# Scores inside the feature weights of a graph-attention kernel's set-up, and its first six adjacency steps prepared in the last set-up block

## The chip, the cores and the metric

The kernel runs on one core of a Trainium2 chip. The metric is the device time of one execution in microseconds. The engines are called PE (TensorE matmul), PEld (its weight loads), DVE (VectorE), ACT (ScalarE), POOL (GpSimd) and SP (SyncE). DMA transfers are issued from the queues of SP, ACT and POOL.

## What is computed

There are 4096 nodes with 512 features and a dense 0/1 adjacency matrix A. Two residual layers follow one another; the change touches the set-up of the first, a graph attention with 8 heads of 64 features.

```python
feats   = einsum('nf,hfo->hno', X, W)              # 8 heads x 64
s_self  = einsum('hno,ho->hn', feats, a_self)
s_neigh = einsum('hno,ho->hn', feats, a_neigh)
dense   = leaky_relu(s_self[:, :, None] + s_neigh[:, None, :], 0.2) * A
attn    = softmax(dense, axis=-1)
out     = relu(einsum('hij,hjo->hio', attn, feats) + b)   # then (N, 512)
x       = layernorm(x + out)
# second layer: attention inside 32 diagonal blocks of 128 nodes, again with
# a residual and a layernorm
```

## The kernel before

The work falls into a set-up (about the first 165 us) and four main passes, one for each pair of heads (`main_pass(0)` to `main_pass(3)`); the second layer runs in pieces between the steps of the last pass. PE's instructions stand in the order of the program (`manual_schedule`). The other engines' orders and those of the DMA queues are made by a scheduler from the program order and its own estimates.

**Set-up.** It goes over the 32 tiles of 128 nodes in eight blocks `k` of four tiles `u`. `load_rows(k)` (L608) brings four tiles of x on SP's queue, into a pool of four buffers. `turn_rows(k)` transposes them on PE (L652, 16 transposes) and ACT copies the result to `xT_f` (L655). `features(k, u)` (L734) multiplies a tile by the feature weights `w_sb_f`: four fp32 matmuls with 128x128 weights and 512 columns, which the trace shows as eight passes. DVE adds the bias from PSUM (L742). The head scores take a way of their own: `scores(k)` (L663) multiplies the transposed block by `wa`, the products of W with `a_self` and `a_neigh`; ACT copies the result to `st` (L671); `exponentials(k)` (L677) brings it back to columns by matmuls with `stack`, and takes five exps on ACT (L686 to L691) and some small bf16 parts on DVE (L694 to L708). `rows_of_exponentials` (L713) and `columns_of_exponentials` (L726) turn the results for later use: the rows go to DRAM as `pu_d`. `scaled_features(k, u)` makes two staging tiles, `gst` (features times an exponential, L748) and `fst` (features split into two float32r parts, L756 on ACT and L757 on DVE), each from a pool of three buffers, and stores them to `g_d` and `f_d` on POOL's queue (L769). The pools of PSUM are seven banks `ps_set` for the set-up and one `ps_m`. After blocks 3, 4 and 5 a part of A is loaded and cast to 8-bit floats on POOL's queue (`load_adjacency`, L587).

**Main pass.** A step `j` is one of 32 rows of tiles, for a chunk `c` of 1024 columns; passes 0 to 2 take eight steps at a time. In pass 0 `bring(0, c, j)` transposes two steps of A on PE (L1113, 16-bit pairs, into `ps_m`), ACT casts each to a float32r tile `at` (L1117), and POOL's queue stores it to `at_d` (L1118); later passes load `at_d` back. For a step DVE makes two tiles `q` (L1367: max, then product), ACT or DVE a `mark` from each (L1376, L1372), and PE sums `accf` (L1387, `at` by `f_s`), `acc` (L1407, `q` by `g_s`), `dens` (L1421, `mark` by `e_b`) and in pass 0 `ae` (L1331). `f_s` and `g_s` are loaded from `f_d` and `g_d`. The tiles `at` and `q` come from pools of 6, to which `ring` adds the further pools `more_at` (6) and `more_q` (2) in passes 0 to 2. At the very first step the pass itself calls `bring` for its eight steps.

Of the kernel before, what the change touches and what calls it, by code (L numbers as in the profile page):

```python
# [19 lines left out]
P = 128  # L20
# [384 lines left out]
def adjacency_streamed_path(  # L405
# [50 lines left out]
    const = ctx.enter_context(tc.tile_pool(name="fconst", bufs=1))  # L456
    first_pass = ExitStack()
# [25 lines left out]
    for c in range(FC):  # L483
# [6 lines left out]

    stack = const.tile([P, 2 * H], F32, name="stack")
    nc.vector.tensor_reduce(
        stack,
        ident.rearrange("p (c k) -> p k c", c=FC)[:, : 2 * H, :],
        AX.X,
        OP.add,
    )
# [56 lines left out]
    more = {}  # L554

    def ring(name, pool, n):

        if name not in more:
            return pool
        k = turns[name] % (n + more[name][1])  # L560
        turns[name] += 1
        return pool if k < n else more[name][0]

    def partial_sums(dst, wide, rhs):

        for c in range(FC):
            nc.tensor.matmul(
                dst[32 * c : 32 * c + 32, :], wide[:, c, :32], rhs[:, c, :], start=True, stop=True
            )
# [21 lines left out]

    with tc.tile_pool(name="setup1", bufs=1, side="right") as one, tc.tile_pool(
        name="setup2", bufs=2, side="right"
    ) as two, tc.tile_pool(name="setup3", bufs=3, side="right") as three, tc.tile_pool(
        name="xtp", bufs=4, side="right"
    ) as xtp, tc.tile_pool(name="ps_setup", bufs=7, space=PSUM) as pss:
        NB = NT // 4
        xts, xTs, sts, pu_js, rows = {}, {}, {}, {}, {}
# [13 lines left out]
        w_sb = one.tile([P, FC, H * FH], F32, name="w_sb_f")  # L612
        for c in range(FC):
            nc.scalar.dma_start(
                w_sb[:, c].rearrange("p (h o) -> p h o", h=H),
                W[:, ts(c, P), :].rearrange("h p o -> p h o"),
            )
        a_b2 = three.tile([P, PR, 2, FP], F32R, name="fst").bitcast(F32)
        a_b2 = a_b2.rearrange("p r s n -> p (r s n)").rearrange(
            "p (k h o) -> p k h o", k=2, h=H  # L620
        )
# [11 lines left out]
        wa = one.tile([P, FC, 32], F32, name="wa")  # L633
        nc.vector.memset(wa, 0.0)
        for c in range(FC):
            for k in range(2):
                prod = three.tile([P, H, FH], F32, name="fb")
                nc.vector.tensor_mul(
                    prod, w_sb[:, c].rearrange("p (h o) -> p h o", h=H), a_b2[:, k]
                )  # L640
                nc.vector.tensor_reduce(wa[:, c, k * H : (k + 1) * H], prod, AX.X, OP.add)
        xs = one.tile([P, FC, NB], F32, name="xs")

        def turn_rows(k):
# [4 lines left out]
            for u, c in order if k == 0 else sorted(order, key=lambda x: x[1]):  # L649
                if u == 0:  # L650
                    pts[c] = pss.tile([P, 4, P], F32, name="ps_set")
                nc.tensor.transpose(pts[c][:, u, :], xts[k][u][:, ts(c, P)], ident)  # L652
# [6 lines left out]
        def scores(k):  # L659

            ps = pss.tile([P, 4 * P], F32, name="ps_set")
            for c in range(FC):
                nc.tensor.matmul(  # L663
                    ps[32 * c : 32 * c + 32, :],
                    wa[:, c, :],
                    xTs[k][:, c].rearrange("p u n -> p (u n)"),
                    start=True,
                    stop=True,
                )
            st = sts[k] = one.tile([P, 4 * P], F32, name="st")  # L670
            nc.scalar.copy(st, ps)  # L671

        def exponentials(k):
            blk = slice(4 * k, 4 * k + 4)
            pts = pss.tile([P, 4, 2, H], F32, name="ps_set")
            for u in range(4):
                nc.tensor.matmul(  # L677
                    pts[:, u].rearrange("p k h -> p (k h)"),
                    tile_j(sts[k], u),
                    stack,  # L680
                    start=(u == 0),
                    stop=True,
                    skip_group_check=True,
                )
            s_c, t_c = pts[:, :, 0, :], pts[:, :, 1, :]
            nc.scalar.activation(e_all[:, blk, 1, :], t_c, AF.Exp)  # L686
            nc.scalar.activation(e_all[:, blk, 0, :], t_c, AF.Exp, scale=ALPHA)
            nc.scalar.activation(d_all[:, blk, :], t_c, AF.Exp, scale=ALPHA - 1.0)
            pu_j = pu_js[k] = two.tile([P, 4, 2, H], F32, name="pu_j")
            nc.scalar.activation(pu_j[:, :, 1, :], s_c, AF.Exp, scale=-ALPHA)  # L690
            nc.scalar.activation(pu_j[:, :, 0, :], s_c, AF.Exp, scale=1.0 - ALPHA)  # L691


# [16 lines left out]
        def rows_of_exponentials(k):  # L710
# [5 lines left out]
            row = rows[k] = one.tile([2 * H, 4 * P], F32, name="pu_row")  # L716
# [14 lines left out]
        def features(k, u):  # L731
            pf = pss.tile([P, H * FH], F32, name="ps_set")
            for c in range(FC):
                nc.tensor.matmul(  # L734
                    pf,
                    tile_j(xTs[k][:, c].rearrange("p u n -> p (u n)"), u),
                    w_sb[:, c, :],
                    start=(c == 0),
                    stop=(c == FC - 1),
                )  # L740
            fb = three.tile([P, H, FH], F32, name="fb")
            nc.vector.tensor_add(fb.rearrange("p h o -> p (h o)"), pf, b_row)  # L742
            return fb

        def scaled_features(k, u, fb):
            j = 4 * k + u
            gst = three.tile([P, PR, 2, FH], F32, name="gst")
            nc.vector.tensor_tensor(  # L748
                gst.rearrange("p r h o -> p (r h) o"),
# [4 lines left out]
            fst = three.tile([P, PR, 2, FP], F32R, name="fst")  # L754
# [10 lines left out]
            for dst, n, src in (  # L765
                (g_d, FP, gst.rearrange("p r h o -> p r (h o)")),
                (f_d, 2 * FP, fst.rearrange("p r s n -> p r (s n)").bitcast(F32)),
            ):
                nc.gpsimd.dma_start(dst[:, k, :, ts(u, n)].rearrange("r p n -> p r n"), src)  # L769

        turn_rows(0)
        for k in range(NB):
            if k + 1 < NB:
                load_rows(k + 1)
            fbs = [features(k, 0)]
            if k == 0:
                fbs.append(features(k, 1))
                scores(0)
            else:
                exponentials(k)  # L780
            if k + 1 < NB:
                turn_rows(k + 1)
            if k == 0:
                exponentials(0)
            scaled_features(k, 0, fbs[0])
            if k:
                fbs.append(features(k, 1))
                columns_of_exponentials(k - 1)
            scaled_features(k, 1, fbs[1])
            fbs.append(features(k, 2))  # L790
            scaled_features(k, 2, fbs[2])
            if k + 1 < NB:
                scores(k + 1)
            rows_of_exponentials(k)
            if k == NB - 1:
                xsum = one.tile([P, FC], F32, name="xsum")
                nc.vector.tensor_reduce(xsum, xs, AX.X, OP.add)
                xsum_b = one.tile([P, FC, 32], F32, name="xsum_b")
# [730 lines left out]
```

## Time and profile before

| | us |
|---|---|
| median of three runs | 2074.67 (2074.32 to 2076.41) |
| the profiled execution, its own time | 2074.4 |
| its span, first to last instruction | 2072.1 |
| PE busy in it | 2040.3 |
| DVE busy | 1663.9 |
| ACT busy | 1536.7 |

The mean granted TensorE clock is 0.996. The profile is of one execution. Busy times overlap between engines. A row of a group gives the line, engine and operation, the tiles written and read, and the count. In the chain of waits each piece is what the end of the program is traced back to. A fp32 matmul of the program stands as two records.

### The profile page before, as it was taken

How to read it: one execution, taken by the hardware profiler on the slowest of the kernel's cores; microseconds unless marked ns; L12 is line 12 of the kernel's file. 1: busy time of each engine (PE TensorE's matmuls, PEld its weight loads, DVE VectorE, ACT ScalarE, POOL GpSimd, SP SyncE). 2: the span in 40 equal slices, each digit the busy share in tenths (PEclk: the TensorE clock that was granted, in tenths of full speed). 3: DMA queues.
4: the chain of work that ended last, by engine and by line, in shares of the span. 5: the costliest groups of instructions: out<-in, count | busy, mean ns of one | idle time of the engine just before them, and what ended most of it. 6: DMA issues, size and time to landing. Idle time of an engine off the chain costs nothing.

```text
span 2072.1 us, 37981 instructions
## 1 busy us (share of the span) xinstructions
PE 2040.3 (98%) x14934; PEld 999.7 (48%) x14934; DVE 1663.9 (80%) x2058; ACT 1536.7 (74%) x1821; POOL 247.5 (12%) x393
## 2 busy tenths in 40 slices
PE   8999999999999999999999999999999999999997
PEld 4555555444445444444445444544454444545443
DVE  5557888888799998798999999999975984885654
ACT  3338898888878899788889889998885666567420
POOL 2343222222100000000000000000210210210111
PEclk9999999999999999999999999999999999999999
DMA  8999999999899999788999899989974763775211
GB/s 252 265 258 248 272 293 265 296 261 297 264 332 349 361 334 338 261 312 300 315 318 337 312 342 327 325 292 361 325 234 144 245 243 132 227 272 168 71 49 43
DMA packets 207881, 551.28 MB, mean 266 GB/s; under 512 B 25292, under 2 KB 66252, under 8 KB 207692
## 3 DMA queue, kind: packets, MB, share of 16 engines
q1 hardware_dynamic: 140748, 425.79, 59.4%
q0 software_dynamic: 62784, 121.91, 23.4%
q8 instruction: 119, 1.95, 0.4%
q10 hardware_dynamic: 4160, 1.05, 0.2%
q14 instruction: 70, 0.57, 0.1%
HBM read 491.79 MB, written 107.22 MB: 289 GB/s over the span
## 4 chain that ended last, share of the span: by engine, by line
PE 81%; DMA 8%; issue 5%; DVE 3%; ACT 2%; POOL 1%; POOLq 0%; SPq 0%; DVEq 0%; ACTq 0%
PE acc L1407 35%; PE accf L1387 20%; DMA at_d<-at 5%; PE ps_m L1050 5%; PE ps_m L978 5%; PE dens L1421 5%; PE ps_set L734 4%; DVE q L1367 1%; PE ps_m L1005 1%; PE ps_m L1064 1%; ACT mark L1376 1%; DMA xt_f<-in_x_dram 1%; PE ps_m L907 1%; PE ps_m L1113 1%; PE ps_m L958 1%
## 5 line engine op out<-in xcount | busy, mean ns | idle before, releaser
L1367 DVE SCALAR_TENSOR_TENSOR q<-p_row,d_all,at 128x1024 f32<-128x1024 f32 x1024 | 1242.6, 1280 | 159.2 <-PE acc L1407 130.1
L1376 ACT ACTIVATE mark<-q,nb_all 128x1024 fp8e4<-128x1024 f32 x896 | 994.2, 1145 | 173.1 <-DVE q L1367 158.1
L1407 PE MATMUL acc<-q,g_s 128*32 128x512 f32 x8192 | 903.3, 593 | 1.1 <-DVE q L1367 0.4
L1407 PEld LDWEIGHTS acc<-q,g_s 128*32 128x32 f32 x8192 | 264.6, 110 | 594.5 <-issue 533.7
L1387 PE MATMUL accf<-at,f_s 128*128 128x512 f32 x2048 | 493.3, 397 | 1.9 <-issue 1.8
L1387 PEld LDWEIGHTS accf<-at,f_s 128*128 128x128 f32 x2048 | 379.3, 188 | 110.6 <-issue 29.1
L1132 ACT ACTIVATE ck<-ck,neg_half_f 128x1024 f32<-128x1024 f32 x128 | 146.0, 1140 | 22.1 <-DMA ck<-in_adj_dram 22.1
L1133 ACT ACTIVATE ck<-ck,neg_quarter 128x1024 f32<-128x1024 f32 x128 | 146.3, 1143 | 1.9
L1117 ACT CAST at<-ps_m 128x1024 fp32r<-128x1024 fp8e4 x128 | 120.2, 1025 | 8.7 <-PE ps_m L1113 5.6
L1421 PE MATMUL dens<-mark,e_b 128*6 128x512 fp8e4 x2048 | 124.4, 379 | 0.7 <-ACT mark L1376 0.7
L734 PE MATMUL ps_set<-w_sb_f,xT_f 128*128 128x512 f32 x256 | 117.3, 607 | 0.1
L978 PE MATMUL ps_m<-x1T,M_sb 128*128 128x512 f32 x256 | 113.1, 595 | 1.6 <-ACT x1T L959 1.6
L1050 PE MATMUL ps_m<-wvT,x1T 128*128 128x512 f32 x256 | 114.2, 594 | 0.0
L1252 POOL DMA_DIRECT2D hs_d<-hst x12 | 10.7, 894 | 834.0 <-DVE hst L1242 740.0
L1372 DVE TENSOR_SCALAR mark<-q,d_all 128x1024 fp8e4<-128x1024 f32 x128 | 96.0, 750 | 5.1 <-DVE q L1367 0.5
L1421 PEld LDWEIGHTS <-e_b 128*6 128x6 bf16 x2048 | 52.8, 86 | 80.4 <-issue 37.0
L1118 POOL DMA_DIRECT2D at_d<-at x128 | 68.8, 538 | 170.5 <-ACT at L1117 106.9
L756 ACT ACTIVATE fst<-fb 128x512 fp32r<-128x512 f32 x32 | 20.3, 636 | 83.9 <-DVE fb L742 52.9
L978 PEld LDWEIGHTS ps_m<-x1T,M_sb 128*128 128x128 f32 x256 | 47.9, 190 | 63.0 <-issue 59.9
L1050 PEld LDWEIGHTS ps_m<-wvT,x1T 128*128 128x128 f32 x256 | 47.6, 190 | 57.2 <-issue 56.0
L985 ACT ACTIVATE zT<-ps_m,zb 128x512 f32<-128x512 f32 x32 | 21.8, 683 | 71.0 <-PE ps_m L978 71.0
L734 PEld LDWEIGHTS ps_set<-w_sb_f,xT_f 128*128 128x128 f32 x256 | 49.2, 200 | 51.5 <-issue 50.2
(185 smaller groups left out, 1117.9 us busy)
## 6 DMA issues: line engine op xcount, KB each, us to landing
at<-at_d SPq DMA_DIRECT2D x384, 512.0 KB, 6.1
ck<-in_adj_dram SPq DMA_DIRECT2D x128, 512.0 KB, 5.5
f_s<-f_d SPq DMA_DIRECT2D x128, 512.0 KB, 7.3
at_d<-at POOLq DMA_DIRECT2D x128, 512.0 KB, 14.9
g_s<-g_d SPq DMA_DIRECT2D x128, 256.0 KB, 5.7
f_d<-fst POOLq DMA_DIRECT2D x32, 512.0 KB, 8.5
p_row<-pu_d SPq DMA_DIRECT2D x32, 512.0 KB, 6.9
a_b<-in_adj_dram POOLq DMA_DIRECT2D x32, 512.0 KB, 16.4
```

What stands on the lines that cost most here:

```text
L734: nc.tensor.matmul(pf, tile_j(xTs[k][:, c].rearrange("p u n -> p (u n)"), u), w_sb[:, c, :], start=(c == 0), stop=(c == FC - 1),)
L978: nc.tensor.matmul(pz, L1["M"][:, f, ts(c, P)], x1T[:, f, :], start=(f == 0), stop=(f == FC - 1),)
L1050: nc.tensor.matmul(pv, x1T[:, f, ts(u, P)], L1["wvT"][:, f, :], start=(f == 0), stop=(f == FC - 1),)
L1117: nc.scalar.copy(at, both[:, :, k])
L1132: tc.keep_in_program_order(nc.scalar.activation(ck, ck, AF.Square, bias=neg_half))
L1133: nc.scalar.activation(ck, ck, AF.Abs, bias=neg_quarter, accum_out=binp[:, k : k + 1])
L1367: nc.vector.scalar_tensor_tensor(q, p_row[h], d_j, ats[r, c, j].bitcast(F32), op0=OP.max, op1=OP.mult)
L1372: nc.vector.tensor_scalar(mark, q, d_j, None, op0=OP.is_gt, saturate=False)
L1376: nc.scalar.activation(mark, q, AF.Sigmoid, bias=nb_all[:, j, hh : hh + 1], scale=BIG, saturate=False,)
L1387: nc.tensor.matmul(accf[:, s, :], f_s[j // 4][:, j % 4, w, :], ats[r, c, j][:, ts(s, HB)], start=(j == 0 and w == 0), stop=(j == NT - 1 an ...
L1407: nc.tensor.matmul(acc[o : o + 32, s, :], g_s[j // 4][:, j % 4, h, o % FH : o % FH + 32], qs[j, h][:, ts(s, HB)], start=(j == 0), stop=(j ...
L1421: nc.tensor.matmul(dens[lo : lo + 6, :], e_b[:, j, 2 * r + h, :], marks[j, h][:, ts(s, HB)], start=(j == 0), stop=(j == NT - 1),)
```

## The change

- The scores become part of the feature weights: `w_sb_f` has 66 columns for each head, 64 of features and two of scores (the sums over W times `a_self` and `a_neigh`). A tile's product is then 528 columns wide and lies in two PSUM banks (`ps_fe`, two buffers of two banks; `ps_set` keeps three). Each of the four matmuls is split into two of 264 columns. `scores`, the copy `st`, and the matmuls with `stack` are gone. The exps are taken for each tile from PSUM by two small DVE products with `powers` and three exps on ACT. The first three tiles are multiplied without the score columns, and get their scores from 12 small matmuls in `first_scores`.
- The two staging tiles of `scaled_features` come from the main pass's pools `q` (`both`: the biased features and `gst`) and `at` (`fst`), six buffers each. Their stores are issued on SP's queue.
- `rows_of_exponentials(k)` and `columns_of_exponentials(k)` run in the next block; those of the last block follow its last tile.
- `more_at` is opened before the set-up and used first by `ring`. In the last block `early_steps` calls `bring` for the steps 0 to 5 of the first pass, after the features of tiles 0, 1 and 2.

```diff
-    more = {}
+    more = {"at": (at2, MORE)}
...
-            return pool
-        k = turns[name] % (n + more[name][1])
+            return pool
+        pool_2, m = more[name]
+        k = turns[name] % (n + m)
         turns[name] += 1
-        return pool if k < n else more[name][0]
+        if name == "at":
+            return pool_2 if k < m else pool
+        return pool if k < n else pool_2
...
-    ) as xtp, tc.tile_pool(name="ps_setup", bufs=7, space=PSUM) as pss:
+    ) as two, tc.tile_pool(name="xtp", bufs=4, side="right") as xtp, tc.tile_pool(
+        name="setup_rows", bufs=1, side="right"
+    ) as late, tc.tile_pool(name="ps_setup", bufs=3, space=PSUM) as pss, tc.tile_pool(
+        name="ps_feat", bufs=2, space=PSUM
+    ) as psf:
...
         for c in range(FC):
+            prod = qp.tile([P, C], F32, name="q").rearrange("p (k h o) -> p k h o", k=2, h=H)
             for k in range(2):
+                nc.vector.tensor_mul(prod[:, k], w_sb[:, c, :, :FH], a_b2[:, k])
+                nc.vector.tensor_reduce(w_sb[:, c, :, FH + k], prod[:, k], AX.X, OP.add)
...
-        def scores(k):
-            ps = pss.tile([P, 4 * P], F32, name="ps_set")
-            for c in range(FC):
-                nc.tensor.matmul(
-                    ps[32 * c : 32 * c + 32, :],
-                    wa[:, c, :],
-                    xTs[k][:, c].rearrange("p u n -> p (u n)"),
-                    start=True,
-                    stop=True,
-                )
-            st = sts[k] = one.tile([P, 4 * P], F32, name="st")
-            nc.scalar.copy(st, ps)
...
+        def exponentials(k, u, sc):
+            j = 4 * k + u
+            if u == 0:
+                pu_js[k] = two.tile([P, 4, 2, H], F32, name="pu_j")
+            st = small.tile([P, 5, H], F32, name="st")
+            for lo, hi, w in ((0, 3, 1), (3, 5, 0)):
+                nc.vector.tensor_tensor(
+                    st[:, lo:hi].rearrange("p k (q h) -> p k q h", q=2),
+                    sc[:, None, :, :, w].to_broadcast([P, hi - lo, 2, H // 2]),
+                    powers[:, lo:hi].rearrange("p k (q h) -> p k q h", q=2),
+                    OP.mult,
+                )
+            nc.scalar.activation(e_all[:, j], st[:, 0:2], AF.Exp)
+            nc.scalar.activation(pu_js[k][:, u], st[:, 3:5], AF.Exp)
+            nc.scalar.activation(d_all[:, j, :], st[:, 2], AF.Exp)
...
         def features(k, u):
-            pf = pss.tile([P, H * FH], F32, name="ps_set")
+            pf = psf.tile([P, 2, HB], F32, name="ps_fe")
+            pf = pf[:, :, : H * FW // 2].rearrange("p q (h w) -> p q h w", w=FW)
+            scored = k > 0 or u == 3
+            cols = slice(0, FW if scored else FH)
             for c in range(FC):
-                nc.tensor.matmul(
-                    pf,
-                    tile_j(xTs[k][:, c].rearrange("p u n -> p (u n)"), u),
-                    w_sb[:, c, :],
...
+                for q in range(2):
+                    nc.tensor.matmul(
+                        pf[:, q, :, cols],
+                        tile_j(xTs[k][:, c].rearrange("p u n -> p (u n)"), u),
+                        w_sb[:, c, 4 * q : 4 * q + 4, cols],
...
+            both = qp.tile([P, C], F32, name="q").rearrange("p (s h o) -> p s h o", s=2, h=H)
...
+            if scored:
+                exponentials(k, u, pf[:, :, :, FH:])
+            return both
...
-            fst = three.tile([P, PR, 2, FP], F32R, name="fst")
+            fst = atp.tile([P, C], F32R, name="at").rearrange(
+                "p (r s n) -> p r s n", r=PR, s=2
+            )
...
-                nc.gpsimd.dma_start(dst[:, k, :, ts(u, n)].rearrange("r p n -> p r n"), src)
+                nc.sync.dma_start(dst[:, k, :, ts(u, n)].rearrange("r p n -> p r n"), src)
...
+        def early_steps(k, u):
+            if k == NB - 1 and u < 3:
+                bring(0, 0, 2 * u)
...
+            for u in range(4):
+                fbs[u] = features(k, u)
+                early_steps(k, u)
+                if u == (0 if k else 2) and k + 1 < NB:
+                    turn_rows(k + 1)
+                if u == 1 and k:
+                    rows_of_exponentials(k - 1)
+                if u == 2 and k:
+                    columns_of_exponentials(k - 1)
+                if u == 2 and k == 0:
+                    first_scores()
+                    for v in range(3):
+                        scaled_features(k, v, fbs[v])
+                if k or u == 3:
+                    scaled_features(k, u, fbs[u])
...
+            parts_of_exponentials(k)
...
                 if at_step == 0:
                     for j in cycle:
-                        bring(0, 0, j)
+                        if (0, 0, j) not in ats:
+                            bring(0, 0, j)
```

## The prediction

> **What bounds the kernel now.** I read the page's busy shares and chain of waits first, then a table of windows cut at the blocks of the set-up, then the chain and the timelines inside them. The page:
>
> ```profile
> PE 2040.3 (98%) x14934; PEld 999.7 (48%) x14934; DVE 1663.9 (80%) x2058; ACT 1536.7 (74%) x1821; POOL 247.5 (12%) x393
> PE 81%; DMA 8%; issue 5%; DVE 3%; ACT 2%; POOL 1%; POOLq 0%; SPq 0%; DVEq 0%; ACTq 0%
> ```
>
> TensorE is the bound nearly everywhere, so a microsecond taken off its set-up should reach the end. The windows (span, then busy time of PE, PEld, DVE, ACT and POOL with counts, clock, DMA share, GB/s) run from one block's second `features` call to the next; the last is the step from set-up into the main pass.
>
> ```profile
> 39.45:58.10 18.65, 18.65 (x75) 9.70 (x74) 10.24 (x27) 6.49 (x22) 6.67 (x10) 1.00 0.91 262
> 95.35:113.80 18.45, 18.45 (x74) 9.51 (x73) 7.33 (x15) 4.19 (x10) 5.70 (x8) 1.00 1.10 245
> 161.55:178.20 16.65, 13.91 (x97) 11.50 (x97) 12.74 (x15) 14.90 (x16) 7.60 (x12) 0.79 0.86 293
> ```
>
> A block costs 18.5 us with PE full, DVE and ACT half idle, and the DMA rings near full. The boundary has 2.7 us of PE idle and a clock of 0.79. One block in the chain of waits (start, us, what):
>
> ```profile
> 95.35 3.44 PE ps_set L734 x8
> 98.79 0.35 PE ps_set L726 x4
> 99.14 3.64 PE ps_set L734 x8
> 102.78 1.00 PE ps_set L663 x8
> 103.78 0.54 PE ps_set L713 x4
> 104.31 6.88 PE ps_set L734 x16
> 111.19 0.84 PE ps_set L677 x8
> 112.03 1.79 PE ps_set L652 x16
> ```
>
> It adds to 18.48: four feature tiles 13.96 (a tile is eight fp32 passes of 512 columns, 3.44, or 3.64 after a matmul of another weight shape), scores 1.00, `stack` 0.84, transposes 1.79, rows 0.54, columns 0.35.
>
> **The feature passes.** Each becomes two of 264 columns (256 of features, 8 of scores), with the 128x128 weights loaded twice as often; 512 columns show no price for that. The weight loads' timeline in the last pass (start, us) has three neighbours:
>
> ```profile
> 1703.18 0.19 PEld L978 LDWEIGHTS ps_m<-x1T,M_sb 128*128 128x128 f32 x1 [0.24 <-issue]
> 1703.61 0.19 PEld L978 LDWEIGHTS ps_m<-x1T,M_sb 128*128 128x128 f32 x1 [0.24 <-issue]
> 1713.68 3.52 PEld L1387 LDWEIGHTS accf<-at,f_s 128*128 128x128 f32 x16
> 1718.23 1.86 PEld L1005 LDWEIGHTS ps_m<-x1T,zT 128*128 128x128 f32 x16
> ```
>
> L978 streams 512 fp32 columns, one pass per 0.43. L1005 streams 128: (1.86-0.19)/15 = 0.111 a pass, so a 0.19 us load hides behind even that. A line through the two gives 0.224 at 264 columns. L1387, one pass per (3.52-0.19)/15 = 0.222, has the same load behind about as long a stream. Bounds: 0.220 (a straight share of 0.43) and 0.239 (L1387's mean over the page is 493.3/2048 = 0.241, with group changes in it). I take 0.224: a tile costs 16 x 0.224 = 3.58, 0.14 more than 3.44. The two ends move the set-up by 32 x 16 x (-0.004 to +0.015) = -2 to +8.
>
> The Trainium skill (TensorE: Matmul & The Clock Gate, LDWEIGHTS) gives a load of P columns P/1.2 ns, 107 for these, and its section on the back-to-back gap lets load and matmul together set the spacing, which speaks against halving the stream. Were 0.107 only half hidden, a pass would cost 0.28 and the set-up 27 us more; L1005's 0.111 with a load each time disagrees, so the trace decides.
>
> **A block.** Gone: scores 1.00 and `stack` 0.84. New: 4 x 0.14 = 0.57, and 0.2 for a second tile that follows another weight shape (after the rows; after the columns it was there). The 24 exps and products of a block are small: exps of 128x32 took 0.20 on ACT (6.5 of 18.6 busy), products are bounded by the 0.16 to 0.22 of DVE's small rows, eight of them 1.6 on an engine at 10. They hide behind the next tile's 3.6 us. So does the staging in `at` and `q` tiles: with three buffers ACT waited 23.1 us for `f_d` transfers without moving PE, and now there are six. With three `ps_set` buffers the fourth transpose group waits for ACT's first copy (0.60, started 0.65 after the first group): 0 to 0.2, I take nothing. So 18.48 - 1.84 + 0.57 + 0.2 = 17.4; six blocks save 6 x 1.05 = **6.3**.
>
> **The head.** Until the eighth weight product (20.1) PE now waits too, for `features(0,2)` needs the bank that the first addition on DVE frees (product rows end about 19.6, addition 0.69: 20.4). Then 3.5 + 1.8 (transposes) + 24 score passes of 16 columns at 0.112 (the `stack` rows: 0.84 for 8) 2.7 + 3.7 + 3.6 + 1.8 = 37.5 to 37.9 against 39.45 before: **-1.6**, bounds -2.2 to 0.
>
> **The last block.** From 148.96 to 161.55 it took 12.59. Now three tiles 10.74, rows 0.54, columns 0.35, L567 0.99, three weight-shape changes 0.6, three `bring` groups at 0.62 (the L1113 x8 of the chain) 1.9: 15.1, **+2.5**. Their six casts (1.02 each, 6.1 us) go to ACT, which was busy 3.4 of 12.6 there; without that cover each pair would hold the single `ps_m` bank for 2 us more. End of features: 161.55 - 1.6 - 6.3 + 2.5 = 156.1.
>
> **The boundary.** PE's timeline of before:
>
> ```profile
> 165.77 1.01 PE L1113 MATMUL ps_m<-ident_b,a_b 128*128 128x128 bf16 x8 [1.83 <-ACT at L1117]
> 167.60 1.01 PE L1113 MATMUL ps_m<-ident_b,a_b 128*128 128x128 bf16 x8 [0.82 <-ACT at L1117]
> 168.37 8.96 PE L1387 MATMUL accf<-at,f_s 128*128 128x512 f32 x32
> ```
>
> These waits go, but another comes: `rows_of_exponentials(7)` now stands behind the last tile and waits for its addition 0.69, two products 0.3, ACT's copy 0.63 and two exps 0.3, about 1.9 us of PE idle. Behind it are L574, the columns and `accf`. PE would be through `accf` 12 to 14 us after the features instead of 15.6 (14 if the clock halves again; 0.79 over 16.65 lost 3.4). But DVE is late next: after the additions and small parts (about 7 us) it owes 15 q of 1.28 and two marks of 0.75, ending 27.4 after the features, and the last `acc` needs 1.8 more: 29.2 against 192.3 - 161.55 = 30.75 before. Gain **1.5**, bounds 0 to 3.6.
>
> **Sum.** 1.6 + 6.3 - 2.5 + 1.5 = 6.9 off the profiled execution's 2074.4 (span 2072.1 and 2.3 around it), which stands 0.3 under the median: 2067.5, and as median 2067.8. In the main passes the order of all five engines is the same but for a few moved operations in the last pass (up to 1 us either way).
>
> **Rival 1, the loads of x come late (slower).** The 64 stores of g and f leave POOL's queue for SP's, where the xt_f loads stand between them. Each store waits there for DVE or ACT; behind a waiting store stand the next xt_f loads, and for those PE's transposes. SP's order puts the fourth xt_f behind `f_d` of the same block's first tile (copies and casts: about 3.6 us after the transposes). DMA issues at 95 to 114 us (count, KB, median us to landing):
>
> ```profile
> xt_f<-in_x_dram SPq DMA_DIRECT2D x6, 256.0 KB, 9.5
> f_d<-fst POOLq DMA_DIRECT2D x3, 512.0 KB, 14.0
> g_d<-gst POOLq DMA_DIRECT2D x4, 256.0 KB, 12.3
> ```
>
> Cover is 17.4 - 1.8 = 15.6. Issue 3.6 late plus 9.5 is 13.1: hidden, which I take. Plus the stores' own 14.0 it is 17.6: 2 us of PE wait in each of three blocks; the longest xt_f landing of before, 15.9, makes it 3.9. Four blocks at 2 to 4 us lose 8 to 16; at 12 the time is 2067.8 + 12 = 2079.8. Landings beyond 12 us start it, and from 11 us of waits (6.9 and the 4.1 below) it ends slower. POOL's packets of 4 KB may also shrink to the 512 B and 1 KB rows of the stores; the only small ones here (W, 256 B, 18 ns) move 14 bytes a ns against 23 for POOL's (4096 B in 174 ns), at the worst 5 us of ring time more for a block's 3.1 MB. For: DMA share 0.80 to 1.10. Against: six staging buffers instead of three, and no store of SP's needs a GpSimd turn of 0.75.
>
> The Trainium skill (DMA: Bandwidth & Descriptors, Queues, rings and completion order) says that an engine serves its queue rows in turn. By it the loads had a turn to themselves and now stand in line behind up to seven DMAs, which speaks against this change; the landings of 9.5 beside stores of 14.0 agree with it.
>
> **Rival 2, the narrow pass costs 0.235 to 0.239.** Loss 6 to 8 of the 6.9: 2073.5 to 2075.5, no change. L1387's mean speaks for it, L1005 against.
>
> **Rival 3, the gain is given back at the boundary and in the first groups**, because DVE's run of q starts later than I think: 3 to 4 us gone, 2071 to 2072, inside the band of no change.
>
> **How the numbers follow.** Forecast 0.56 (2063 to 2070); rivals 2 and 3 together 0.20; rival 1 0.24, a sixth of it still inside the band below. A measurement of this kernel tells about 0.2%, 4.1 us, from no change. So faster 0.56, same 0.24, slower 0.20. Low end: 0.220 a pass (-2) and 2 more at the boundary, 2063. The high end takes in rivals 2 and 3 and somewhat under half of rival 1: 2079.
>
> **What would show it.** Right: in the chain, feature tiles of x16 at 3.55 to 3.65; blocks of 17.4; PE idle of 2 us before the rows of block 7; `accf` beginning near 161; the DVE run ending near 184. Wrong: PE waits in the transposes put down to DMA xt_f (rival 1); feature tiles of 3.8 (rival 2); PE waiting for DVE q in the first `acc` group for more than 2 us (rival 3).

## The result, and the profile after

The change makes the kernel slower: 2085.38 us (2080.75 to 2088.07, six runs) beside 2074.49 for the kernel before in the same session, a ratio of 1.0047 (95% interval 1.0036 to 1.0058). The profiled execution took 2085.67, its span is 2083.8. Forecast were 2067.8 and a range up to 2079.0.

The page after, busy times and shares of the chain of waits:

```profile
PE 2038.5 (98%) x15086; PEld 1047.4 (50%) x15086; DVE 1667.3 (80%) x2125; ACT 1542.8 (74%) x1869; POOL 192.5 (9%) x329
PE 81%; DMA 7%; issue 5%; DVE 4%; ACT 2%; POOL 1%; POOLq 0%; SPq 0%; DVEq 0%; ACTq 0%
```

PE is busy 1.8 us less than before in a span 11.7 us longer: the edit saves PE work, and PE waits 13.5 us more. (Part of the saving is hidden by the clock, see below.) The windows show where (columns as before: stretch, its length, busy PE, PEld, DVE, ACT, POOL with counts, clock, DMA share, GB/s):

```profile
39.20:56.38 17.18, 17.18 (x90) 14.77 (x89) 10.48 (x32) 6.63 (x26) 0.78 (x1) 1.00 1.05 296
92.34:117.62 25.28, 19.14 (x90) 16.19 (x89) 10.74 (x33) 7.50 (x29) 1.43 (x2) 0.87 1.11 263
165.61:185.37 19.76, 13.55 (x74) 10.87 (x72) 14.13 (x28) 11.69 (x15) 2.50 (x4) 0.74 1.12 267
```

An undisturbed block lasts 17.18, less than the 17.4 of the forecast. But one takes 25.28, with 6 us of idle PE, at a DMA share of 1.11. The last row is the boundary, from the last feature pass to the first `acc`. In the last two rows the granted clock is below 1. These are the stretches up to 200 us in which it was halved, three in the kernel after, then the only one in the kernel before:

```profile
29.10:32.50 3.40, 3.40 (x9) 2.65 (x9) 2.47 (x5) 1.23 (x8) 0.00 (x0) 0.51 0.88 292
111.10:117.90 6.80, 3.58 (x15) 3.29 (x16) 0.69 (x1) 2.29 (x10) 0.00 (x0) 0.50 1.05 247
169.10:179.30 10.20, 5.92 (x23) 4.92 (x24) 5.61 (x18) 6.54 (x7) 2.50 (x4) 0.50 1.09 359
```

```profile
164.50:171.30 6.80, 4.71 (x23) 3.97 (x23) 6.35 (x7) 6.77 (x8) 3.98 (x7) 0.50 0.91 322
```

Half of PE's busy time in them is an estimate of what they cost: 6.5 us after, 2.4 before. So at the full clock the edit saves some 5.9 us of PE work, not 1.8, and of the 11.7 us about 4.1 are clock; the second and third stretch lie at waits of PE that are described next. The chain of waits inside the long block (start, us, what):

```profile
90.58 13.02 DMA f_d<-at
...
103.62 0.02 SPq L628
103.66 11.09 DMA xt_f<-in_x_dram
...
114.80 3.03 PE ps_set L670 x13
```

SP's load of the fourth `xt_f` waits for the end of an `f_d` store that stands eight places ahead of it on SP's queue, and then takes 11.09 us itself. The number eight is the program's: in the trace the DMAs of SP and ACT use eight completion semaphores in turn, and each is issued only when the one before it on its semaphore has landed (that store landed at 103.60, the load was issued at 103.66). The waits from 92 to 175 us (who waited for whom, us in total, times, longest) hold this and the boundary:

```profile
PE ps_set L670 <- DMA xt_f<-in_x_dram: 7.1, 4, 3.0
ACT pu_row L719 <- DMA pu_d<-pu_row: 5.2, 1, 5.2
PE ps_set L728 <- ACT pu_row L719: 4.8, 1, 4.8
```

The last two were in no step of the prediction: the copy into `pu_row` (one buffer) for block 7 waits until the `pu_d` store of block 6 has landed. That store was issued on POOL's queue at 159.10, behind `at_d` stores and an `a_b` load, and took 13.55 us.

### The profile page after: what moved, and what is told of

The parts are those of the page before. It is cut to its first block, busy times and chain, and to the rows that moved or that the text cites. A ratio compares the mean times of both kernels' runs of the same rounds, so it can differ in the third digit from the quotient of the medians.

```text
span 2083.8 us, 38356 instructions
## 1 busy us (share of the span) xinstructions
PE 2038.5 (98%) x15086; PEld 1047.4 (50%) x15086; DVE 1667.3 (80%) x2125; ACT 1542.8 (74%) x1869; POOL 192.5 (9%) x329
## 3 DMA queue, kind: packets, MB, share of 16 engines
q10 hardware_dynamic: 4160, 1.05, 0.2%
## 4 chain that ended last, share of the span: by engine, by line
PE 81%; DMA 7%; issue 5%; DVE 4%; ACT 2%; POOL 1%; POOLq 0%; SPq 0%; DVEq 0%; ACTq 0%
PE acc L1422 37%; PE accf L1402 21%; PE ps_m L1085 5%; PE dens L1436 5%; PE ps_m L1013 5%; DMA at_d<-at 3%; DVE q L1382 2%; PE ps_fe L740 2%; PE ps_m L1040 1%; PE ps_m L1099 1%; DMA xt_f<-in_x_dram 1%; ACT mark L1391 1%; PE ps_m L603 1%; PE ps_m L942 1%; DMA pu_d<-pu_row 1%
## 5 line engine op out<-in xcount | busy, mean ns | idle before, releaser
L740 PE MATMUL ps_fe<-w_sb_f,xT_f 128*128 128x264 f32 (+1 forms) x512 | 122.1, 395 | 2.2 <-DVE q L748 2.0
L740 PEld LDWEIGHTS ps_fe<-w_sb_f,xT_f 128*128 128x128 f32 x512 | 100.7, 201 | 17.2 <-DVE q L748 2.4
L1266 POOL DMA_DIRECT2D hs_d<-hst x12 | 10.7, 893 | 841.0 <-DVE hst L1256 727.1
L1093 DVE TENSOR_TENSOR v_t<-ps_m,bv_row 128x512 f32<-128x512 f32 x32 | 21.9, 686 | 61.8 <-PE ps_m L1085 61.8
## 6 DMA issues: line engine op xcount, KB each, us to landing
a_b<-in_adj_dram POOLq DMA_DIRECT2D x32, 512.0 KB, 15.3
```

Of the source, the lines that this page charges most:

```text
L740: nc.tensor.matmul(pf[:, q, :, cols], tile_j(xTs[k][:, c].rearrange("p u n -> p (u n)"), u), w_sb[:, c, 4 * q : 4 * q + 4, cols], start=(c ...
```

## The experiments

All places are us from the span's start, each kernel's profiled execution. "Lead" is the start of an `accf` group minus that of the same group before; negative is ahead. "Step" is how much longer the first group of main pass 3 lasts than before. "Half clock" is what the stretches of halved clock cost PE by the estimate above, without the one at the program's end that every run has. Ratios are of medians, places of one execution: the profiled ones of e7 and e13 took 2082.07 and 2080.17 us beside medians of 2077.87 and 2078.13, so their leads stand too high by that much.

| kernel | ratio to before (95%) | features(1,1) | features(7,1) | features end | accf | lead, second group | lead, pass 3 | step | lead, last group | half clock |
|---|---|---|---|---|---|---|---|---|---|---|
| before | | 39.5 | 148.8 | 161.6 | 168.4 | | | | | 2.4 |
| after | 1.0047 (1.0036 to 1.0058) | 39.2 | 151.8 | 165.8 | 174.7 | 7.2 | 8.5 | 2.8 | 12.0 | 6.5 |
| e1 stores on POOL | 0.9986 (0.9978 to 0.9995) | 39.3 | 143.4 | 157.3 | 161.4 | -6.7 | -5.9 | 2.5 | -3.6 | 3.4 |
| e2 own row buffer | 1.0096 (1.0077 to 1.0115) | 39.4 | 152.7 | 166.7 | 170.7 | 14.6 | 16.5 | 5.2 | 20.8 | 8.9 |
| e3 x loads on ACT | 1.0076 (1.0062 to 1.0089) | 42.5 | 157.0 | 171.0 | 180.2 | 11.8 | 15.3 | 3.5 | 18.2 | 10.2 |
| e4 before, stores on SP | 0.9992 (0.9983 to 1.0001) | 39.8 | 148.8 | 161.6 | 168.4 | 0.0 | 0.9 | 0.0 | 0.4 | 2.4 |
| e5 long store runs | 1.0053 (1.0039 to 1.0066) | 37.7 | 143.6 | 157.6 | 171.0 | 2.7 | 7.1 | 4.7 | 11.5 | 5.6 |
| e6 POOL, pools exchanged | 0.9969 (0.9957 to 0.9981) | 39.3 | 143.3 | 157.3 | 161.4 | -7.5 | -4.6 | 0.0 | -5.5 | 1.7 |
| e7 POOL, no early steps | 1.0001 (0.9992 to 1.0010) | 39.8 | 145.5 | 158.5 | 166.8 | -1.7 | 4.2 | 3.0 | 7.4 | 7.3 |
| e8 long runs, pu_d on ACT, exchanged | 1.0056 (1.0042 to 1.0070) | 53.5 | 154.8 | 168.8 | 172.8 | 4.7 | 9.7 | 0.0 | 9.5 | 4.2 |
| e9 pu_d on ACT | 1.0107 (1.0091 to 1.0122) | 53.5 | 154.8 | 168.8 | 172.8 | 15.1 | 17.8 | 3.0 | 21.5 | 3.7 |
| e10 pools exchanged | 1.0035 (1.0021 to 1.0048) | 37.4 | 147.7 | 161.6 | 170.6 | 2.4 | 5.3 | 0.0 | 5.1 | 4.7 |
| e11 as e8, two pu_d on ACT | 1.0004 (0.9995 to 1.0013) | 39.6 | 144.1 | 158.1 | 162.2 | -6.0 | 1.3 | 0.0 | 0.9 | 5.1 |
| e12 e11, hst on SP | 1.0052 (1.0037 to 1.0068) | 39.1 | 145.4 | 159.4 | 163.4 | -6.3 | 12.1 | 0.0 | 13.4 | 8.0 |
| e13 e6, hst on SP | 1.0008 (0.9999 to 1.0017) | 39.4 | 145.2 | 159.2 | 163.5 | -3.9 | 6.7 | 0.0 | 6.4 | 8.5 |

**Stores back on POOL's queue (e1).**

```diff
-                nc.sync.dma_start(dst[:, k, :, ts(u, n)].rearrange("r p n -> p r n"), src)
+                nc.gpsimd.dma_start(dst[:, k, :, ts(u, n)].rearrange("r p n -> p r n"), src)
```

> The changed kernel with one line put back: the stores of g and f are issued on POOL's queue again. In the changed kernel the span from features(1,1) to features(7,1) is 112.6 us (39.20 to 151.79); its two undisturbed blocks take 17.17, so six would take 103.0, and 9.6 us are lost. Theory 1 (the stores in SP's queue hold back the loads of x): the blocks come back to 17.2 to 17.5, features(7,1) starts at 142 to 144, PE waits in the transposes for xt_f fall from 13.7 to 6 or less, and the time falls by 8 to 10, to about 2076. Rival (the DMA rings themselves are full, so a block cannot be much under the 18.5 us of before wherever its stores are issued): features(7,1) not before 149, the time not under 2083.

Theory 1 in the set-up: `features(7,1)` at 143.4, `accf` at 161.4 where the prediction had 161. The ratio falls by 0.0061, 12.7 us of 2074.5, more than the 8 to 10 of the blocks: the six blocks take 104.1 instead of 112.6, and from the features' end to `accf` it is 4.0 instead of 8.9. PE's timeline of the boundary (start, us, group, idle time before it and what ended it):

```profile
157.18 0.49 PE L715 MATMUL ps_set<-ident_f,pu_j 128*16 128x128 f32 x3
159.05 0.28 PE L715 MATMUL ps_set<-ident_f,pu_j 128*16 128x128 f32 x1 [1.38 <-ACT pu_j L691]
...
161.40 4.84 PE L1402 MATMUL accf<-at,f_s 128*128 128x512 f32 x13 [0.38 <-DVE pu_all L729]
```

The wait of 1.38 for the exps is the 1.9 foreseen, and the wait for `pu_row` is gone too. The result holds for the queue and for the packets, which changed together; the next three runs part them.

**Loads of x on ACT's queue (e3).**

```diff
-                nc.sync.dma_start(xt, x[ts(4 * k + u, P), :])
+                (nc.scalar if k else nc.sync).dma_start(xt, x[ts(4 * k + u, P), :])
```

> The changed kernel with the loads of x for blocks 1 to 7 issued on ACT's queue; the stores of g and f stay on SP's queue, with their packets of 512 B and 1 KB. It tells the order in one queue from the size of the packets. Theory 1a (the loads stand behind the stores in one queue): the waits of PE for xt_f fall below 6 us, features(7,1) starts at 142 to 145, the time falls by 7 to 10, to 2076 to 2078. Theory 1b (small packets and full rings make the loads late whichever queue they are in): landings of xt_f stay at 9 to 13 us, features(7,1) after 149, the time 2083 to 2086.

The loads landed sooner (6.0 us in the median, 7.7 at most), which 1b had not expected, and the kernel was slower still, which 1a had not. The chain between 76 and 102 us says why:

```profile
74.56 11.81 DMA g_d<-q
86.39 0.34 ACTq L628
```

The load's issue on ACT waited for the end of a store of `g_d` with the same semaphore, and ACT's copies and exps waited behind it (15.2 us in two waits). Moving the load to another queue moved the stall.

**Stores on SP's queue alone (e4),** the same line in the kernel before:

> The kernel before with one line of the change alone: its stores of g and f are issued on SP's queue. Theory 1: the blocks with loads of A are lengthened here too, but a block of 18.5 us covers 1.3 us more than one of 17.2, so the loss is smaller than the 9.6 us of the changed kernel: features(7,1) at 151 to 156 instead of 148.96, the time up by 2 to 7, 2077 to 2081. Rival (the stores only hurt together with the staging in the at and q buffers or the shorter blocks): features(7,1) within 1 us of 148.96 and the time within 2 us of 2074.5.

The rival: nothing lost. So neither the queue nor the small packets cost anything while a block lasts 18.5 us.

**Long runs for the stores, still on SP's queue (e5).**

```diff
-    g_d = dram.tile([PR, NT // 4, P, 4 * FP], F32, name="g_d")
-    f_d = dram.tile([PR, NT // 4, P, 4 * 2 * FP], F32, name="f_d")
+    g_d = dram.tile([NT // 4, P, 4, PR, FP], F32, name="g_d")
+    f_d = dram.tile([NT // 4, P, 4, PR, 2 * FP], F32, name="f_d")
...
-                nc.sync.dma_start(dst[:, k, :, ts(u, n)].rearrange("r p n -> p r n"), src)
+                nc.sync.dma_start(dst[k, :, u], src)
```

> The changed kernel, its stores still on SP's queue, with g_d and f_d laid out in DRAM so that a partition's part of a store is one run of 2 KB or 4 KB (the loads of the main passes then read runs of 512 B and 1 KB). It tells the packets of the stores from their place in the queue. From 40 to 145 us the packets of the stores took 60.5 us of the sixteen DMA engines' time in the changed kernel (46 and 27 ns for 1 KB and 512 B) and 53.5 with the stores on POOL's queue (165 ns for 4 KB), beside 50 to 52 of other traffic; six blocks of 17.17 last 103. Theory P (the DMA engines' time is the bound there, and small packets push it over what the blocks leave): the stores' share falls to about 54, features(7,1) comes at 143 to 147 instead of 151.8, the time at 2075 to 2080. Rival Q (the stores' place in front of the loads of x in one queue): features(7,1) not before 150, the time 2083 to 2087. In the main passes smaller packets of the loads should cost nothing, as they are far from full; if they do, the spacing of the accf groups shows it.

For the set-up this decides for theory P: with the stores where the change put them, `features(7,1)` comes at 143.6, as with POOL (the six blocks take 105.9, and the head, whose clock was not halved, is 1.5 us shorter). The time does not follow, since the wait for `pu_row` is now 9.3 us (`accf` 13.4 after the features) and the step of pass 3 is 4.7, 1.7 of it half clock. The main passes, which I had called "far from full", have a DMA share of 0.97 before and 1.00 here (200 to 1360 us). The DMA queues from `features(1,1)` to `features(7,1)` (queue, packets, MB, share of 16 engines), after, then e1, then e5; q1 is fed by SP, q0 by POOL:

```profile
q1 hardware_dynamic: 29004, 28.05, 87.0%
q0 software_dynamic: 3312, 1.77, 17.1%
```

```profile
q0 software_dynamic: 8291, 19.22, 70.9%
q1 hardware_dynamic: 4192, 9.44, 29.1%
```

```profile
q1 hardware_dynamic: 12470, 27.95, 75.2%
q0 software_dynamic: 3312, 1.77, 18.6%
```

About the same 29 to 30 MB, in 32324, 12492 and 15790 packets. Share times stretch gives the packets' time on an engine: 1.041 x 112.6 = 117 us after, 1.000 x 104.1 = 104 in e1, 0.938 x 105.9 = 99 in e5. PE needs 101.3 for the six blocks (the last has no transposes), as e9, of which more below, shows (columns as before):

```profile
53.49:154.77 101.28, 101.28 (x522) 87.28 (x521) 61.96 (x190) 39.78 (x147) 0.00 (x0) 1.00 0.96 280
```

In e4 it is 1.048 x 109.0 = 114, in the 109 us that its longer blocks leave, at the same share of 1.04 to 1.05. Packet times overlap, since a share can pass 1; so 114 in 109 cost nothing, and 117 in 101 could not be had. With the stores in small packets all runs with short blocks and loads of A among them (after, e2, e3, e10) ended at a share of 1.02 to 1.06. The small packets ask for more time than the shortened blocks have. (These packet times were taken under that load; they are no demand measured apart.)

**A row buffer of its own (e2), and pu_d on ACT's queue (e9).**

```diff
+            if k == NB - 1:
+                row = rows[k] = evp.tile([P, C], F32, name="ys")[: 2 * H, : 4 * P]
```

> The changed kernel with a buffer of its own for the last block's pu_row (taken from the buffer ys, which the main pass first uses at the end of its first chunk), so that ACT's copy of block 7 no longer waits until the pu_d store of block 6 has been read out. Theory 2 (this wait is the one on the path at the boundary): PE's wait of 4.83 us before the columns is gone, accf begins near 170 instead of 174.7, and the time falls by 4 to 5, to about 2081. Rival (DVE's run of q sets the first acc group in any case): accf begins earlier, but acc of the first group starts less than 2 us earlier, and the time stays within 2 us of 2085.4.

```diff
-            nc.gpsimd.dma_start(pu_d[:, ts(k, 4 * P)], row)
+            nc.scalar.dma_start(pu_d[:, ts(k, 4 * P)], row)
```

> The changed kernel with one edit: the stores of pu_d are issued on ACT's queue instead of POOL's. It asks again what the run with a second row buffer could not answer, since there the order of SP's queue changed as well. Theory 2 (block 7's copy into pu_row waits for the landing of the pu_d store of block 6, late on POOL's queue): the wait of 4.8 us before the columns is gone, accf begins 4 to 5 us earlier against the features' end (8.9 us after it in the changed kernel, 4 here), and the time is 4 to 5 us under that of the changed kernel: a ratio to the kernel before of 1.0023 to 1.0030 instead of 1.0047. Rival (DVE's run of q takes the gain): a ratio of 1.004 or more.

Both take the wait away: `accf` begins 4.0 us after the features' end instead of 8.9. Neither gains, for a reason that neither theory had. The waits of e9:

```profile
DVE q L1382 <- DMA g_d<-q: 12.2, 2, 8.0
PE acc L1422 <- DVE q L1382: 5.7, 1, 5.7
```

DVE's first tiles `q` use the buffers in which the last `both` tiles lay, and wait until the last `g_d` stores have landed; with PE on time this wait is laid open. In e2, moreover, SP issued that store only at 174.32, behind a load of `bv_row` before which the queue had stood for 7 us. And e9 shows a second side effect: with no `pu_d` on POOL's queue, nothing held back the three `a_b` loads. They ran in the first 30 us (26 us to landing), W came late, and `features(1,1)` 14 us late. Its six blocks, now without those loads (in the change 17.1% of 112.6, 19 us), ran at 16.9 us each, small packets and all: theory P once more.

**The pools of at exchanged (e6 with stores on POOL, e10 alone).**

```diff
-        if name == "at":
-            return pool_2 if k < m else pool
...
-            fst = atp.tile([P, C], F32R, name="at").rearrange(
+            fst = at2.tile([P, C], F32R, name="at").rearrange(
```

> Stores of g and f on POOL's queue as in the run before of that name, and the roles of the two pools for at exchanged: the staging of the set-up takes more_at, the early steps and ring take the at pool first, as the kernel before does; more_at stays opened first and on the right side. In all four runs with more_at used first the first group of main pass 3 took 2.6 to 5.3 us longer than before, with 0 in the run with the stores alone moved. Theory R (the order of the ring: pass 3 has only the at pool for its steps from 4 on, and its six buffers are then held by the last six steps of pass 2, so the reloads are issued late): this step of 2.6 is gone and the time is 2068 to 2070, against 2072.3 with the stores on POOL alone. Rival (the place of more_at in memory, and what the pools of the last pass then lie over): the step stays, 2071 to 2074.

> The changed kernel with one edit: the staging of the set-up takes more_at, the early steps and ring take the at pool first. Theory R: set-up and boundary as in the changed kernel within 1 us, the first group of main pass 3 not longer than before (2.8 us longer in the changed kernel, 3.4 by group 60), a ratio to the kernel before of 1.0030 to 1.0035. Rival: the ratio stays at 1.0045 or more.

The step is 0.0 in every run with the exchange (also e8, e11 to e13) and 2.5 to 5.2 in every run without it but e4, which has the ring of the kernel before (in e2 and e5, the two largest, 1.7 is half clock). Set-up and boundary of e10 were 4 us better than after's, more than the 1 us allowed, 1.7 of it because the head's clock was not halved; so its ratio does not weigh the ring alone. DVE's timeline at the start of pass 3, first of the kernel after, then of e6:

```profile
1374.98 1.22 DVE L1183 TENSOR_TENSOR ys<-ys,acc 128x1024 f32<-128x1024 f32 x1
...
1383.56 0.56 DVE L1162 SCALAR_TENSOR_TENSOR x1b<-hp_l,x1b 128x384 f32<-128x384 f32 x1 [3.77 <-DMA hp_l<-hs_d]
```

```profile
1361.84 1.22 DVE L1181 TENSOR_TENSOR ys<-ys,acc 128x1024 f32<-128x1024 f32 x1
...
1366.56 0.55 DVE L1160 SCALAR_TENSOR_TENSOR x1b<-hp_l,x1b 128x384 f32<-128x384 f32 x1
```

So the order of the ring is the cause, but not by late `at` loads, as I had written: it changes the order of SP's queue, the load of `hp_l` is issued 2.3 us after `ys` begins (0.4 us before it in e6), and DVE waits 3.77 for it with three `q` behind. e6 is the fastest version: 0.9969, 6.4 us of 2074.5. Of its 3.5 us beyond e1 (the intervals overlap slightly), 1.7 are again clock: from the features' end to the first `acc` it takes 12.5 us at 1.00, e1 14.1 with 3.4 us at half.

**No early steps (e7),** with stores on POOL's queue:

```diff
-            if k == NB - 1 and u < 3:
+            if False:
```

> Stores of g and f on POOL's queue, and no early steps: the first pass brings its eight steps itself, as before; more_at is still opened first and used first. Theory (the early steps give what the boundary gained): features end 2 to 2.5 us earlier, near 155, but accf begins near 166 instead of 161.4 after four bring groups of 2 us, and the time is 3 to 5 us above the 2072.3 with early steps, 2075 to 2077. Rival (DVE's run of q sets the first acc group in any case): acc of the first group within 1.5 us of the 171.5 there, the time within 2 us of 2072.3.

As the theory said: `accf` is at 166.8 against 161.4, the second group 5.0 us later than in e1, and the ratio 0.0015 (3.1 us) higher. The features ended 1.2 us later than in e1, not 2 earlier: the two blocks before `features(7,1)` took 1.6 us more, in them 3.4 us at half clock.

**The causes together, stores still on SP (e8, e11).** e8 is e5 with the edits of e9 and e10; e11 moves only the `pu_d` stores of blocks 6 and 7.

> The changed kernel, its stores of g and f still on SP's queue, with three edits together: the layout of g_d and f_d in which a store has runs of 2 KB and 4 KB, the stores of pu_d issued on ACT's queue, and the roles of the two at pools exchanged. If the three causes found so far are the whole loss (packets of the stores; pu_row's only buffer held by a pu_d store that lies on POOL's queue behind at_d and a_b; the order of the at ring), features end at 157 to 158, PE's wait before the columns (9.3 us with the layout alone) is under 1, accf begins at 161 to 162, the first group of main pass 3 is no longer than before, and the time is 5 to 7 us under the kernel before, a ratio of 0.9966 to 0.9976. Rival (the stores' place in SP's queue costs something by itself): a ratio over 0.999.

> The three edits of the run before (store runs of 2 and 4 KB, exchanged roles of the at pools, pu_d off POOL's queue), but only the last two pu_d stores, of blocks 6 and 7, go to ACT's queue. With all eight moved, nothing on POOL's queue held back the three loads of A any more: they ran in the first 30 us and W landed 14 us late (features(1,1) at 53.5 instead of 39.2). Theory (packets, pu_row's buffer and the ring of at are the whole loss, and the stores' place in SP's queue costs nothing by itself): features(1,1) at 37 to 39, features(7,1) at 142 to 144, features end at 157 to 158, accf begins 4 us later near 161.5, the first group of main pass 3 is no longer than before, and the ratio to the kernel before is 0.9962 to 0.9976. Rival (another wait takes the place, such as DVE's q for the last store of g as in the run with all pu_d on ACT's queue): accf begins near 161.5, but the second group starts 5 us or more late against it, and the ratio is 0.9985 or more.

e8 lost its gain to the late W, as e9 did. e11 has set-up and boundary as expected (`accf` at 162.2, second group 6.0 ahead, no step, no wait for `g_d`): the place of the stores on SP's queue costs nothing by itself once their runs are long. But the ratio was missed: 7.2 us go in passes 0 to 2, 5.2 of them between groups 8 and 16 (1.7 of these by half clock). Waits of e11 from 300 to 640 us:

```profile
ACT hst L1188 <- DMA hs_d<-hst: 12.8, 3, 6.3
PE dens L1434 <- ACT mark L1389: 3.0, 5, 0.7
```

**The store of hst (e12, e13).**

```diff
-                nc.gpsimd.dma_start(
+                (nc.gpsimd if r else nc.sync).dma_start(
                     hs_d[ts(c, C), ts(r, FP)].rearrange("(t p) n -> p t n", p=P), hst
```

> The run before (store runs of 2 and 4 KB, the at pools exchanged, the last two pu_d stores on ACT's queue) with one more edit: in the first pass the store of hst to hs_d is issued on SP's queue instead of POOL's. That run was 6.0 us ahead of the kernel before at the second accf group and 1.3 behind at the start of pass 3; 5.2 of it went between groups 8 and 16 of pass 0. Theory H (ACT waits for the landing of the hst store, which lies on POOL's queue among at_d and a_b, and its marks and casts come late: over eight profiles the waits of ACT for hs_d were 8.2 to 8.6 us where nothing was lost there and 11.6 to 12.8 where 3 to 5 us were): ACT's waits for hs_d fall under 6 us in pass 0, groups 8 to 16 lose less than 1, and the ratio to the kernel before is 0.9970 to 0.9985 instead of 1.0004. Rival (a coincidence, the loss comes from the shorter runs of the f_s and g_s loads or from the order of POOL's queue): groups 8 to 16 lose 4 or more again, ratio 0.9995 or more.

> The fastest kernel so far (stores of g and f on POOL's queue, the at pools exchanged; ratio 0.9969) with the same edit, hst stored on SP's queue in the first pass. There ACT's waits for hs_d were 8.6 us and 2.9 us were lost between the second group and pass 3, 0.9 of them between groups 8 and 16. Theory H: up to 1 us less, a ratio of 0.9960 to 0.9970. Rival: SP's loads of u_row and f_s now stand behind this store, which waits for DVE; then the first groups of chunks 1 to 3 start later, by 1 us or more in all, a ratio over 0.9975.

The remedy failed: on SP's queue the store lands after 16.2 us in the median (e12) and 13.1 (e13), on POOL's after 10.5 (e11) and 9.2 (e6). The wait of ACT grew, and the loss with it. Wait and loss from group 8 to 16: 8.2 to 8.6 us and -0.7 to 0.9 (after, e1, e6), 8.5 to 10.5 and 0 to 2.0 (before, e2, e3, e4, e9, e10), 11.6 to 12.8 and 2.9 to 5.2 (e5, e7, e8, e11), 13.1 and 6.8 (e13), 22.2 and 15.2 (e12). Without half clock the losses are 2.7 (e7), 3.5 (e11), 5.1 (e13) and 10.7 (e12). Loss follows the wait in both directions, which speaks for theory H without showing it, as neither edit shortened the wait; in e12 and e13 PE waits for no load of `f_s` or `u_row`, against e13's rival. That e7 loses 4.4 with the old layout speaks against the shorter loads of e12's rival; the order of POOL's queue stays open. Why the store's landing differs among the kernels on POOL's queue was not tried.

## Why the prediction was wrong, by its steps

Up to the second `accf` group the sum forecast 6.9 us ahead; it came 7.2 behind. By its terms, forecast and measured: head -1.6 and -0.2; blocks -6.3 and +3.2; last block +2.5 and +1.2; boundary -1.5 and +3.0. The step that failed is the hiding of the loads of x in the blocks, 9.5 of the 14.1 us; the boundary's is 4.5.

- **The narrow pass: right.** 222 to 223 ns a pass where I took 224; tiles of 3.57. Rival 2 is out. The trace stays with L1005's hidden weight load, against a spacing set by load and matmul together.
- **A block, 17.4: right in size, wrong in cover.** 17.18 undisturbed, and e1 takes 5.3 off the six blocks where the sum had 6.3, one block of 19.9 still waiting for its loads; e9, which never waits there, takes 8.1 off. In the change itself they cost 112.6 instead of 109.4. The failed step is "Issue 3.6 late plus 9.5 is 13.1: hidden, which I take": in the long block its fourth load was issued 11.3 us after the transposes before it and took 11.1, 22.4 against the cover of 15.6. Under it lie the packets: I had their shrinking as a remark in rival 1, "at the worst 5 us" for a block's traffic, and summed nothing over the set-up. It needed a budget: the engines were at a share of 0.80 to 1.10 in the blocks before, about 107 us (98.0% of 109.35) for blocks that were to be shortened to 103, and 512 B in 27 ns and 1 KB in 46 ns (medians) move 19 and 22 bytes a ns where POOL's 4096 B in 165 ns move 25. Rival 1, at 0.24, named the late loads, and its 8 to 16 us were met (112.6 beside 109.4 - 6.3 = 103.1); but it put them down to the queue's order, which e5 and e11 rule out as enough by itself.
- **The head, -1.6: right in its work, missed by the clock,** -0.2. The wait for DVE's addition came as the sum had it (`features(0,2)` at 20.0 instead of 20.4). But from 29.1 to 32.5 the clock was halved, and two feature tiles took 8.9 us where e10 took 7.2 at 1.00. e5 and e10, without this stretch, came to -1.8 and -2.1. PE had stood 2.0 us for the addition in the change, 1.5 and 1.3 in e5 and e10; that this set off the clock is not shown.
- **The last block, +2.5: half of it,** +1.2 in e1 (14.0 against 12.7), counted from `features(7,1)`; one of its three `bring` groups stands ahead of that.
- **The boundary, -1.5: right in its way where it could be seen.** From the features' end to the first `acc` it is 14.1 in e1 against 16.6, a gain of 2.5 inside the bounds. In the change it is 19.6: the term that was left out is the single `pu_row` buffer. The prediction followed the stores past SP's queue, and not `pu_d` behind `at_d` and `a_b` on POOL's. Behind this lay another, the staging in `q` buffers (e2, e9).
- **"In the main passes the order of all five engines is the same": wrong.** The lead goes from 7.2 to 8.5 up to pass 3 and to 12.0 in it, the latter from the changed order of the `at` ring.

The sum itself: with stores on POOL and the pools exchanged the second group is 7.5 ahead where 6.9 was forecast, and the end 5.5. That the sum is met is partly luck: head and blocks fall 1.4 and 1.0 short, last block and boundary gain 1.3 and 1.8 over it, the latter with no half clock. Between the change's last group and that of e6 lie 12.0 + 5.5 = 17.5 us: 8.5 of them before the features' end (165.8 beside 157.3), 4.8 at `pu_row`, 1.4 in the first group, and 2.8 in the passes, with the step of pass 3. The clock has its part in these: 6.5 beside 1.7 us. What e6 itself loses there, from 7.5 to 4.6 ahead before pass 3, is only in part the wait for hst; the rest stays open.

The Trainium skill (DMA: Bandwidth & Descriptors, Issuing engines are not separate DMA queues) says that DMAs from all engines run on the same sixteen DMA engines, and that spreading them gains only issue time. e3 agrees: with the loads on ACT's queue the blocks moved 261 GB/s, beside 266 in the change. The rule that I had cited from the section on queues, with its turns, pointed at the queue and misled me. The same page (Why small descriptors are slow (HBM only)) gives a fixed cost of some three cycles a packet beside 32 bytes a cycle; by that, as an estimate, a 512 B packet would pay 19% and a 1 KB packet 9%. The trace has, by medians, 31% and 11% more time a byte than POOL's 4096 B packets, so measurement decides; but the page's figure, too, adds to traffic that already stood at 107 us.

## What to carry to other kernels

Before a phase is shortened, add up what its DMA traffic takes at the packet sizes it will have, and compare it with the new length: where it is well above, saved engine time is not there to be had (here 117 us did not go into 101; 114 went into 109, so the sum is a warning and no sharp bound). Moving a store to another queue changes its packets as well as its place; look at both, and at what the vacated queue will now let run early or hold back. A buffer shared with a later phase, or with only one copy, is a wait for the transfer that reads it; each one removed can lay open the next. Read the granted clock beside every wait: here 4.1 of the 11.7 us lost were PE's own work at half clock.

## What had not been expected of the hardware

- The stores of this layout went out as 512 B and 1 KB packets from SP's queue, and as 4096 B packets from POOL's, 28508 packets under 2 KB against 4416 for the same traffic.
- Single issues of stores of short runs took up to 3.97 us on SP in the set-up of the change (4.32 in e4), against 0.36 elsewhere. With long runs (e5) or with the stores on POOL (e1) no store or load of x took SP over 0.93, at DMA shares of 0.94 and 1.00. So a high share alone does not do it.
- Three transfers of 512 KB (`a_b`, cast on the way, in 512 B packets of 96 ns in the median), issued one after another in e9, landed after 16.4, 26.1 and 30.8 us beside the head's loads; in the blocks of the change one took 14.
- The clock went to half for 3.4, 6.8 and 10.2 us in the first 180 us of the change, in two of the three around waits of PE of 3.0 and 4.8 us. In e6, with the stores on POOL, one stretch of 3.4 was left.
